# Spreading the position arithmetic of a deformable convolution between its taps

## The chip, the cores and the metric

The kernel runs on one core of one Trainium2 chip. Its engines are TensorE (PE in the profile; PEld is its weight load), VectorE (DVE), ScalarE (ACT), GpSimd (POOL) and SyncE (SP), which here only starts DMAs. The metric is the device time of one execution in microseconds, lower is better. Before the change it is 16,689.37 us, the median of three runs from 16,679.99 to 16,696.37.

## The reference

Four layers are applied one after the other to an array x of 8 images, 64 channels, 128 x 128 pixels, in float32, each as `x = x + layer(groupnorm(x))`. Layer 0 is a modulated deformable 3 x 3 convolution, layer 1 a plain 3 x 3 convolution, layer 2 a two-directional state-space scan, layer 3 a nearest-neighbour block. The change touches layer 0 alone:

```python
offset = conv2d(x, wh, bh, 0, p) + conv2d(x, wv, bv, p, 0)     # 1x15 and 15x1
mask = sigmoid(conv2d(x, wm, bm, 1, 1))                        # 3x3
y = deform_conv2d(x, offset, mask, wd, pad=1)
```

For each pixel and each of nine kernel points, `deform_conv2d` takes the pixel's position plus the offset, reads the four pixels around that place, weights them bilinearly (zero outside the image), multiplies by the mask, and sums over channels and kernel points with `wd`. A batch norm and a ReLU follow.

## The kernel before

Images are handled in pairs, two times 64 channels on 128 partitions, so there are four pairs `p`. Layer 0 first writes the normalized pair into a table in device memory (`fill`), in which one row holds a pixel and the one below it, so that one read of two neighbouring rows returns all four corners of a sampling place.

Then `deform` goes over 16 blocks `e` of eight image rows in each pair. A block is two calls of `sample` of four rows each, and a call is eight groups: four image rows (`m`) times two images (`i`). In one group a partition is a column of the row, and there are nine taps `k`, one for each kernel point. For each tap POOL issues one indirect DMA (L389), which gathers 128 pieces of 256 floats by the indices in `idx` into a `g` tile (four buffers); DVE multiplies them by the corner weights `wts` (L398) and sums the four corners (L399) into `sm`, which has two buffers. Five PE transposes (L403, L405) and two ACT copies (L406, L407) bring `sm` into channel order in `st`, and after eight groups ten PE products with `wd` (L412) give the four rows' result, which SP stores (L416). So a block has 16 groups and 144 gathers, and layer 0 has 64 blocks and 9,216 gathers.

Indices and weights of a block are made during the block before it. The generator `offsets` loads 22 image rows into `xe` (L311; two buffers), normalizes them on ACT (L312), and for each half of the block makes 33 shifted products on PE into `po` (L323), adds the bias on ACT (L333), transposes back (L336) and copies the result into `off` on DVE (L337). It gives way (`yield`) after every sixth product and after each copy. Then `positions` computes from `off`, with 17 DVE operations and one ACT sigmoid (L350 to L372), the clipped positions, their whole and fractional parts, the index `idx` (L364), and the four corner weights (L372). Before the change it is an ordinary function that issues all of these in one go.

What runs between the groups is set by `work`, which `sample` calls after each group. It takes one step of `near`, the `offsets` generator of the next block, and at each third call one step of `far`: the setup of later layers, and statistics and table of the next pair. What is left of `near` runs at the end of the block, what is left of `far` before the last block of a pair. This order of emission goes to a planner, which gives each engine an in-order queue; it keeps to the order of emission as far as operands and buffers are ready in its own estimate, and moves single instructions past each other where they aren't.

The layers after this one (`rest`) start when the last block is done and are not touched.

Of the kernel before, what the change touches and what calls it, by code (L numbers as in the profile page):

```python
# [41 lines left out]
class Net:  # L42
# [134 lines left out]
    def deform(self):  # L177
# [6 lines left out]
        with ExitStack() as ctx:  # L184
# [11 lines left out]
            with tc.tile_pool(name="a_setup", bufs=1) as sp:  # L196
                zeros = sp.tile([P, 2 * PW], F32, name="zeros")
                nc.gpsimd.memset(zeros, 0.0)
                for table in (t for pair in tables for t in pair):
                    flat = table.rearrange("a b q -> a (b q)")  # L200
                    n = LINE * PW // P
# [58 lines left out]
            ready = {}  # L260
# [44 lines left out]
            def offsets(p, e):  # L305

                r, nb = norms[p]
                lo, hi = max(0, 8 * e - 7), min(H, 8 * e + 15)
                xe = ep.tile([P, 22, H], F32, tag="xe", name=f"xe{p}_{e}")
                xf = xe.rearrange("p h w -> p (h w)")[:, 0 : (hi - lo) * H]  # L310
                nc.sync.dma_start(xf, self.x[p * P : (p + 1) * P, lo * H : hi * H])  # L311
                nc.scalar.activation(xf, xf, AF.Identity, bias=nb, scale=r)  # L312
                off = offp.tile([P, 3, 8, 18], F32, tag="off", name=f"off{p}_{e}")
                for g in (2 * e, 2 * e + 1):
                    po = ps_conv.tile([54, 4, H], F32, tag="po", name=f"po{p}_{g}")
                    used = []
                    for t, (dy, dx) in enumerate(taps):
                        r0, r1 = max(0, -dy - 4 * g), min(4, H - dy - 4 * g)
                        if r0 < r1:
                            used.append((t, dy, dx, r0, r1, max(0, -dx), min(H, H - dx)))  # L320
                    for n, (t, dy, dx, r0, r1, c0, c1) in enumerate(used):
                        row = 4 * g + dy - lo
                        nc.tensor.matmul(  # L323
                            po[:, r0:r1, c0:c1],
                            lhsT=wt[:, t, :],
                            rhs=xe[:, row + r0 : row + r1, c0 + dx : c1 + dx],
                            start=n == 0,
                            stop=n == len(used) - 1,
                        )
                        if n % 6 == 5:  # L330
                            yield
                    ob = op.tile([54, 4, H], F32, tag="ob", name=f"ob{p}_{g}")
                    nc.scalar.activation(ob, po, AF.Identity, bias=bias, scale=1.0)  # L333
                    tp = ps_t.tile([P, 4, 3, 18], F32, tag="tp", name=f"to{p}_{g}")
                    for m in range(4):
                        nc.tensor.transpose(tp[:, m].rearrange("p d n -> p (d n)"), ob[:, m, :], self.ident[0:54, 0:54])  # L336
                    nc.vector.tensor_copy(off[:, :, 4 * (g % 2) : 4 * (g % 2) + 4, :].rearrange("p d r n -> p r d n"), tp)  # L337
                    yield
                ready[p, e] = positions(p, e, off)
                yield  # L340

            def positions(p, e, off):

                n = 8 * 18
                h0 = 8 * e
                pos = op.tile([P, 2, n], F32, tag="pos", name=f"pos{p}_{e}")
                cell = op.tile([P, 2, n], F32, tag="cell", name=f"cell{p}_{e}")
                up = op.tile([P, 2, n], F32, tag="up", name=f"up{p}_{e}")
                o = off.rearrange("p d r n -> p d (r n)")
                nc.vector.scalar_tensor_tensor(pos[:, 0], base_y, float(h0), o[:, 0], ALU.add, ALU.add)  # L350
                nc.vector.tensor_add(pos[:, 1], base_x, o[:, 1])

                nc.vector.tensor_scalar(pos, pos, -2.0, float(H), ALU.max, ALU.min)  # L353
                whole = up.bitcast(I32)
                nc.vector.tensor_copy(whole, pos)
                nc.vector.tensor_copy(cell, whole)
                nc.vector.tensor_tensor(up, cell, pos, ALU.is_gt)
                nc.vector.tensor_sub(cell, cell, up)

                nc.vector.tensor_sub(pos, pos, cell)  # L360
                nc.vector.tensor_scalar(up, pos, -1.0, 1.0, ALU.mult, ALU.add)
                idx = wp.tile([P, n], I32, tag="idx", name=f"idx{p}_{e}")
                nc.vector.scalar_tensor_tensor(cell[:, 0], cell[:, 0], float(LINE), cell[:, 1], ALU.mult, ALU.add)
                nc.vector.tensor_scalar_add(idx, cell[:, 0], float(2 * LINE + 2))  # L364
                mask = o[:, 2]
                nc.scalar.activation(mask, mask, AF.Sigmoid)
                nc.vector.tensor_mul(pos[:, 0], pos[:, 0], mask)
                nc.vector.tensor_mul(up[:, 0], up[:, 0], mask)
                w = wtp.tile([P, n, 2, 2], F32, tag="wts", name=f"wts{p}_{e}")
                for b, wx in ((0, up), (1, pos)):  # L370
                    for a, wy in ((0, up), (1, pos)):
                        nc.vector.tensor_mul(w[:, :, b, a], wx[:, 1], wy[:, 0])  # L372
                w = w.rearrange("p n b a -> p n (b a)")
                wts = [w[:, 0 : n // 2], w[:, n // 2 :]]
                return idx, wts

            def sample(p, g, table, idx, wts, work):

                yp = ps_y.tile([P, CH], F32, tag="yp", name=f"yp{p}_{g}")
                flat = [table[i].rearrange("a b q -> (a b) q") for i in range(2)]  # L380
                st = [stp.tile([P, 5, CH], F32, tag="st", name=f"s{p}_{g}_{i}") for i in range(2)]
                for m in range(4):
                    for i in range(2):
                        n0 = m * 18 + 9 * i
                        t = gp.tile([P, 9, 4, C], F32, tag="g", name=f"g{p}_{g}_{i}_{m}")
                        tq = t.rearrange("p k q c -> p k (q c)")
                        for k in range(9):
                            at = (g % 2) * 72 + n0 + k
                            nc.gpsimd.indirect_dma_start(  # L389
                                out=tq[:, k, :],  # L390
                                out_offset=None,
                                in_=flat[i],
                                in_offset=bass.IndirectOffsetOnAxis(ap=idx[:, at : at + 1], axis=0),
                            )
                        sm = wp.tile([P, 9, C], F32, tag="sm", name=f"sm{p}_{g}_{i}_{m}")
                        for k in range(9):
                            w = wts[:, n0 + k, :].unsqueeze(2).to_broadcast([P, 4, C])
                            nc.vector.tensor_mul(t[:, k], t[:, k], w)  # L398
                            nc.vector.tensor_reduce(sm[:, k], t[:, k].rearrange("p q c -> p c q"), axis=mybir.AxisListType.X, op=ALU.add)  # L399
                        sm = sm.rearrange("p k c -> p (k c)")  # L400
                        sp = ps_s.tile([P, 4, P], F32, tag="sp", name=f"sp{p}_{g}_{i}_{m}")
                        for j in range(4):
                            nc.tensor.transpose(sp[:, j, :], sm[:, j * P : (j + 1) * P], self.ident)  # L403
                        s1 = ps_s1.tile([C, P], F32, tag="s1", name=f"s1{p}_{g}_{i}_{m}")
                        nc.tensor.transpose(s1, sm[:, 4 * P :], self.ident)  # L405
                        nc.scalar.copy(st[i][:, 0:4, m * P : (m + 1) * P], sp)  # L406
                        nc.scalar.copy(st[i][0:C, 4, m * P : (m + 1) * P], s1)  # L407
                        work()
                for j in range(5):
                    rows = P if j < 4 else C  # L410
                    for i in range(2):
                        nc.tensor.matmul(yp[i * C : (i + 1) * C, :], lhsT=wd[0:rows, j, :], rhs=st[i][0:rows, j, :], start=j == 0, stop=j == 4)  # L412
                nc.vector.bn_stats(self.ystat[:, p * NCH + g, :], yp)
                ys = op.tile([P, CH], F32, tag="ys", name=f"ys{p}_{g}")
                nc.scalar.copy(ys, yp)
                nc.sync.dma_start(self.y[p][:, g * CH : (g + 1) * CH], ys)  # L416
# [10 lines left out]
            for p in range(self.npair):  # L427
# [4 lines left out]
                for e in range(NCH // 2):  # L432
# [4 lines left out]
                    count = [0]  # L437

                    def work(near=near, far=far, count=count):
                        count[0] += 1  # L440
                        next(near, None)
                        if count[0] % 3 == 0:
                            next(far, None)

                    idx, wts = ready.pop((p, e))
# [933 lines left out]
```

## Time and profile before

| What | Value |
|---|---|
| median of three runs | 16,689.37 us |
| the profiled execution's own time | 16,687.07 us |
| its span | 16,685.0 us |
| start to the first gather | 168 us |
| first gather to last gather (layer 0) | 11,716 us: POOL busy 8,910, DVE 8,600, PE 7,144, ACT 1,240 |
| after the last gather | 4,801 us |
| gathers (L389) | 9,216, median 946 ns, mean 967 ns, data landing 2.7 us after the issue |
| granted TensorE clock | 0.79 of full speed in layer 0, 0.91 after it |

The span is the time from the first to the last instruction of one profiled execution. An engine's busy time is the sum of its instructions' records, and issuing of ordinary DMAs isn't counted in it; the gathers on POOL are. Busy times of different engines overlap and can't be added. In a group's row, the idle time is what its engine spent without work just before these instructions, with the cause that ended most of it; "issue" is a pause that nothing in the profile explains as a wait.

### The profile page before, as it was taken

The page shows a single profiled execution, that of the slowest core. Times are in us where ns is not written, and L with a number is a line of the kernel's source. Part 1 is how long each engine was busy: PE and PEld are TensorE (multiplying, and loading weights), DVE is VectorE, ACT ScalarE, POOL GpSimd, SP SyncE. Part 2 cuts the span into 40 slices and gives each one's busy share as a digit, 9 for nine tenths or more (in the row PEclk, how much of TensorE's full clock was granted, in tenths as well). Part 3 has the DMA queues.
Part 4 walks back from the last instruction along what each step waited for, and adds up shares of the span by engine and source line. Part 5 has one row for each costly group of instructions (what it writes and reads, how often), then busy time and mean ns, then how long its engine had stood idle before and what let it go on. Part 6 is the DMA issues. An engine that isn't in the chain of part 4 may idle for free. (4 is left out here: it accounts for less than half of the span.)

```text
span 16685.0 us, 119663 instructions
## 1 busy us (share of the span) xinstructions
PE 11226.6 (67%) x31864; PEld 4101.4 (25%) x31864; DVE 11600.4 (70%) x27208; ACT 2990.4 (18%) x5596; POOL 10394.8 (62%) x10484
## 2 busy tenths in 40 slices
PE   6766565756576655667566566663489888988896
PEld 1211111111111111111111111111144344444443
DVE  6777777777777777777777777777557557566566
ACT  1101111111110011111000110100144243243342
POOL 4777777777777777777777777777434134043142
PEclk9987787878787787878778788776689899999897
DMA  5334444444433344443333333333322433424223
GB/s 172 120 115 128 133 130 135 136 131 134 137 120 112 114 129 130 135 131 120 112 114 113 118 115 114 118 110 108 118 67 68 148 77 104 112 78 133 85 67 103
DMA packets 900631, 1937.61 MB, mean 116 GB/s; under 512 B 199916, under 2 KB 435828, under 8 KB 876404
## 3 DMA queue, kind: packets, MB, share of 16 engines
q0 software_dynamic: 442368, 1208.55, 24.4%
q1 hardware_dynamic: 383204, 684.00, 13.4%
q10 hardware_dynamic: 74384, 37.40, 1.1%
q8 instruction: 260, 4.26, 0.1%
q14 instruction: 415, 3.40, 0.1%
HBM read 1544.92 MB, written 208.10 MB: 105 GB/s over the span
## 5 line engine op out<-in xcount | busy, mean ns | idle before, releaser
L389 POOL DMA_INDIRECT g<-table,idx x9216 | 8908.4, 967 | 2809.5 <-issue 2613.6
L398 DVE TENSOR_TENSOR g<-g,wts 128x256 f32<-128x256 f32 x9216 | 3818.1, 420 | 3101.9 <-DMA g<-table,idx 3084.0
L399 DVE TENSOR_REDUCE sm<-g 128x64 f32<-128x256 f32 x9216 | 4988.3, 580 | 0.8 <-DVE pos L353 0.2
L323 PE MATMUL po<-xe,wt 128*54 128x512 f32 (+3 forms) x8384 | 4734.9, 676 | 44.4 <-ACT ob L333 42.5
L403 PE MATMUL sp<-ident,sm 128*128 128x128 f32 x4096 | 1525.1, 377 | 4117.6 <-DVE sm L399 4100.3
L403 PEld LDWEIGHTS sp<-ident,sm 128*128 128x128 f32 x4096 | 626.2, 155 | 6897.7 <-DVE sm L399 4964.4
L406 ACT COPY s<-sp 128x512 f32<-128x512 f32 x1024 | 600.0, 586 | 8514.1 <-PE sp L403 8514.1
L323 PEld LDWEIGHTS po<-xe,wt 128*54 128x54 f32 x8384 | 929.9, 140 | 1417.2 <-issue 1069.3
L840 POOL COPY l_yb<-ln_y 128x512 f32<-128x512 f32 x128 | 79.1, 659 | 1303.9 <-PE l1v L834 1161.4
L412 PE MATMUL yp<-s,wd 128*64 128x512 f32 (+1 forms) x2560 | 808.1, 652 | 12.6 <-ACT s L406 12.6
L1206 POOL TENSOR_TENSOR u<-u,v 128x512 f32<-128x512 f32 x256 | 330.7, 1292 | 697.4 <-DVE v L1205 519.7
L563 PE MATMUL c<-room,l_w 128*64 128x508 f32 (+1 forms) x3072 | 741.3, 597 | 21.1 <-DMA room<-nx 14.9
L1298 POOL TENSOR_TENSOR ms<-ms,ln_y 128x512 f32<-128x512 f32 x256 | 278.4, 1107 | 738.8 <-DVE ln_y L119 706.7
L1188 ACT ACTIVATE fx<-room,ln_b,ln_g 128x512 f32<-128x512 f32 x512 | 639.2, 1293 | 116.2 <-DMA in<-fx 97.9
L405 PE MATMUL s<-ident,sm 128*64 128x128 f32 x1024 | 345.9, 338 | 363.1 <-DVE sm L399 336.1
L1221 DVE TENSOR_TENSOR_SCAN z<-tabs,z,u 128x256 f32<-128x256 f32 x512 | 444.9, 902 | 208.3 <-POOL u L1206 192.9
L1199 PE MATMUL pv<-in,tabs 128*128 128x512 f32 x1024 | 537.2, 649 | 46.2 <-DVE u L1205 46.2
L1268 PE MATMUL py<-x,outs 128*128 128x512 f32 x1024 | 506.0, 599 | 4.6 <-POOL x L1253 4.2
L1268 PE MATMUL py<-in,outs 128*128 128x512 f32 x1024 | 505.7, 606 | 1.6 <-ACT h L1270 1.2
L1285 PE MATMUL pc<-outs,h 128*128 128x256 f32 x2048 | 498.9, 394 | 9.9 <-DVE h L1271 8.8
L1253 POOL TENSOR_TENSOR x<-x,xt 128x512 f32<-128x512 f32 x256 | 350.6, 1370 | 126.3 <-DVE xt L1252 126.0
L1285 PEld LDWEIGHTS pc<-outs,h 128*128 128x128 f32 x2048 | 382.5, 195 | 168.7 <-issue 65.4
(406 smaller groups left out, 10008.7 us busy)
## 6 DMA issues: line engine op xcount, KB each, us to landing
g<-table,idx POOLq DMA_INDIRECT x9216, 2.7
in<-fx SPq DMA_DIRECT2D x1024, 128.0 KB
xe<-in_x_dram SPq DMA_DIRECT2D x56, 1408.0 KB
table<-q SPq DMA_DIRECT2D x256, 256.0 KB
xs<-in_x_dram SPq DMA_DIRECT2D x32, 1024.0 KB
xt<-in_x_dram SPq DMA_DIRECT2D x32, 1024.0 KB
y<-ys SPq DMA_DIRECT2D x128, 256.0 KB
room<-in_x_dram SPq DMA_DIRECT2D x64, 512.0 KB
```

The costliest lines, as they stand in the source:

```text
L323: nc.tensor.matmul(po[:, r0:r1, c0:c1], lhsT=wt[:, t, :], rhs=xe[:, row + r0 : row + r1, c0 + dx : c1 + dx], start=n == 0, stop=n == len(u ...
L389: nc.gpsimd.indirect_dma_start(out=tq[:, k, :], out_offset=None, in_=flat[i], in_offset=bass.IndirectOffsetOnAxis(ap=idx[:, at : at + 1], ...
L398: nc.vector.tensor_mul(t[:, k], t[:, k], w)
L399: nc.vector.tensor_reduce(sm[:, k], t[:, k].rearrange("p q c -> p c q"), axis=mybir.AxisListType.X, op=ALU.add)
L403: nc.tensor.transpose(sp[:, j, :], sm[:, j * P : (j + 1) * P], self.ident)
L406: nc.scalar.copy(st[i][:, 0:4, m * P : (m + 1) * P], sp)
L412: nc.tensor.matmul(yp[i * C : (i + 1) * C, :], lhsT=wd[0:rows, j, :], rhs=st[i][0:rows, j, :], start=j == 0, stop=j == 4)
L563: nc.tensor.matmul(o, lhsT=lt, rhs=mv, start=k < 2, stop=k >= len(calls) - 2)
L1188: nc.scalar.activation(fx[:, e].rearrange("p h (o m) -> p h o m", m=self.INNER), src[:, e::2], AF.Identity, bias=w["ln1_b"], scale=w["ln1_g"])
L1199: nc.tensor.matmul(pv, lhsT=tabs[:, at : at + P], rhs=fx[:, :, h, :], start=h == 0, stop=h == 1)
L1268: nc.tensor.matmul(py, lhsT=lt, rhs=mv, start=n == 0, stop=n == len(calls) - 1)
L1285: nc.tensor.matmul(pc[:, i], lhsT=hs[:, h, i, m * P : (m + 1) * P], rhs=self.outs[:, CEN : MIX + P], start=True, stop=True)
```

## The change

`positions` becomes a generator that gives way after each of its DVE operations, 17 times in all, and `offsets` runs it with `yield from`. `offsets` itself gives way after every third product, no longer every sixth. `sample` no longer calls `work` after each group but after taps 2, 5 and 8 of each group, inside the loop over taps: 48 calls in a block where there were 16. `far` takes a step at each ninth call in place of each third. No operation is added, removed or altered.

```diff
-                        if n % 6 == 5:
+                        if n % 3 == 2:
                             yield
...
-                ready[p, e] = positions(p, e, off)
+                ready[p, e] = yield from positions(p, e, off)
                 yield
...
                 nc.vector.scalar_tensor_tensor(pos[:, 0], base_y, float(h0), o[:, 0], ALU.add, ALU.add)
+                yield
                 nc.vector.tensor_add(pos[:, 1], base_x, o[:, 1])
+                yield
...
                 for b, wx in ((0, up), (1, pos)):
                     for a, wy in ((0, up), (1, pos)):
                         nc.vector.tensor_mul(w[:, :, b, a], wx[:, 1], wy[:, 0])
+                        yield
...
                             nc.vector.tensor_mul(t[:, k], t[:, k], w)
                             nc.vector.tensor_reduce(sm[:, k], t[:, k].rearrange("p q c -> p c q"), axis=mybir.AxisListType.X, op=ALU.add)
+                            if k % 3 == 2:
+                                work()
...
                         nc.scalar.copy(st[i][0:C, 4, m * P : (m + 1) * P], s1)
-                        work()
...
-                        if count[0] % 3 == 0:
+                        if count[0] % 9 == 0:
                             next(far, None)
```

More of the change, by code (lines that the diff above doesn't have):

```diff
@@ L350, in positions @@
                 nc.vector.scalar_tensor_tensor(pos[:, 0], base_y, float(h0), o[:, 0], ALU.add, ALU.add)
+                yield
                 nc.vector.tensor_add(pos[:, 1], base_x, o[:, 1])
+                yield
                 nc.vector.tensor_scalar(pos, pos, -2.0, float(H), ALU.max, ALU.min)
+                yield
                 whole = up.bitcast(I32)
                 nc.vector.tensor_copy(whole, pos)
+                yield
                 nc.vector.tensor_copy(cell, whole)
+                yield
                 nc.vector.tensor_tensor(up, cell, pos, ALU.is_gt)
+                yield
                 nc.vector.tensor_sub(cell, cell, up)
+                yield
                 nc.vector.tensor_sub(pos, pos, cell)
+                yield
                 nc.vector.tensor_scalar(up, pos, -1.0, 1.0, ALU.mult, ALU.add)
+                yield
                 idx = wp.tile([P, n], I32, tag="idx", name=f"idx{p}_{e}")
                 nc.vector.scalar_tensor_tensor(cell[:, 0], cell[:, 0], float(LINE), cell[:, 1], ALU.mult, ALU.add)
+                yield
                 nc.vector.tensor_scalar_add(idx, cell[:, 0], float(2 * LINE + 2))
+                yield
                 mask = o[:, 2]
@@ L367, in positions @@
                 nc.vector.tensor_mul(pos[:, 0], pos[:, 0], mask)
+                yield
                 nc.vector.tensor_mul(up[:, 0], up[:, 0], mask)
+                yield
                 w = wtp.tile([P, n, 2, 2], F32, tag="wts", name=f"wts{p}_{e}")
@@ L372, in positions @@
                         nc.vector.tensor_mul(w[:, :, b, a], wx[:, 1], wy[:, 0])
+                        yield
                 w = w.rearrange("p n b a -> p n (b a)")
```

## The prediction

> **What bounds the kernel now.** The chip's granted clock and the slices of the page come first: gathers run from the start to slice 29 of 40, and in all of these slices both POOL and DVE show 7 tenths. The question is which of the two waits for the other. The costliest groups of the page (line, engine, operation, out<-in, count, busy us and mean ns, idle before and who ended it):
>
> ```profile
> L389 POOL DMA_INDIRECT g<-table,idx x9216 | 8908.4, 967 | 2809.5 <-issue 2613.6
> L398 DVE TENSOR_TENSOR g<-g,wts 128x256 f32<-128x256 f32 x9216 | 3818.1, 420 | 3101.9 <-DMA g<-table,idx 3084.0
> L399 DVE TENSOR_REDUCE sm<-g 128x64 f32<-128x256 f32 x9216 | 4988.3, 580 | 0.8 <-DVE pos L353 0.2
> ```
>
> DVE waits 3,084 us for gathered data; POOL waits for nearly nothing but its own issue. 8908.4 + 2809.5 = 11,718 us is the stage: the source view of L389 starts the first gather at 167.9 and the last at 11,883.7. That view's waits, by cause:
>
> ```profile
>   issue: 2613.6, 8581
>   DVE sm L399: 142.7, 470
>   DVE g L398: 31.5, 104
> ```
>
> 8,581 of the waits are plain issue of 0.3 us, and the same 0.3 us stands before gathers put down to DVE, so no gather waits for a buffer. POOL is the bound, end to end, and only a shorter gather can shorten the stage. The median gather is 0.946 us, the mean 0.967. I took all 9,215 distances between gather starts from POOL's timeline: the common one is 1.25 us, 9,215 x 1.25 = 11,519, the stage is 197 us longer. So 197 us, 1.2%, is all that can be won here. Where it lies: one block is 144 gathers (16 groups of 9). Groups 14 and 15 of all 64 blocks together carry 114.3 us of it, each other group on average 0.0925 us per block. POOL's timeline in one block at these groups (start, us, idle before):
>
> ```profile
> 6006.01 0.95 POOL L389 DMA_INDIRECT g<-table,idx  x1 [0.30 <-issue]
> 6007.26 0.98 POOL L389 DMA_INDIRECT g<-table,idx  x1 [0.30 <-issue]
> 6008.55 1.33 POOL L389 DMA_INDIRECT g<-table,idx  x1 [0.30 <-issue]
> 6010.18 1.00 POOL L389 DMA_INDIRECT g<-table,idx  x1 [0.30 <-issue]
> 6011.48 1.15 POOL L389 DMA_INDIRECT g<-table,idx  x1 [0.30 <-issue]
> 6012.94 1.37 POOL L389 DMA_INDIRECT g<-table,idx  x1 [0.30 <-DVE sm L399]
> ```
>
> and DVE's at the same time:
>
> ```profile
> 6008.21 0.42 DVE L398 TENSOR_TENSOR g<-g,wts 128x256 f32<-128x256 f32 x1
> 6008.54 0.30 DVE L361 TENSOR_SCALAR up<-pos 128x288 f32<-128x288 f32 x1
> 6008.76 0.30 DVE L363 SCALAR_TENSOR_TENSOR cell<-cell 128x144 f32<-128x144 f32 x1
> ...
> 6010.58 0.57 DVE L399 TENSOR_REDUCE sm<-g 128x64 f32<-128x256 f32 x1
> 6011.07 0.75 DVE L398 TENSOR_TENSOR g<-g,wts 128x256 f32<-128x256 f32 x2
> 6011.74 1.08 DVE L399 TENSOR_REDUCE sm<-g 128x64 f32<-128x256 f32 x2
> 6012.74 0.75 DVE L398 TENSOR_TENSOR g<-g,wts 128x256 f32<-128x256 f32 x2
> ```
>
> The reader is to see two things. While nine position operations run in a row (6008.54 to 6010.58), a gather takes 1.33 us; in other blocks one takes 2.36 to 2.88. Then DVE is behind and runs taps without a pause, two multiplies and two reduces in 1.66 us, and gathers lengthen to DVE's rhythm. In quiet stretches DVE pauses some 0.7 us before every second multiply, and gathers stay at 0.95.
>
> **What the Trainium skill says.** "SBUF — State Buffer", section "Who interferes with whom": a VectorE instruction with two SBUF inputs, or one in a two-port mode (casts and tensor_scalar can be), shares a port pair with GpSimd under an exclusive lock, and a tensor_reduce doesn't. The trace agrees: of 8,359 gathers with a distance under 1.27 us, 5% start while such a DVE operation runs; of 550 with 1.35 to 1.8 us, all do. From phase 0.25 to 0.75 us of a gather they do no harm: there the multiplies lie in most ordinary gathers. "Perfetto Trace Analysis", section "DMA Instruction — SWDGE (GPSIMD)", says a gather's record ends when its descriptors are written, not when data lands; here data land 2.7 us (median) after the issue, so POOL's record is the right measure of its pace. No page prices the order of DVE instructions.
>
> **The change, part by part.**
>
> (a) Positions, 17 DVE operations per block (L350 to L372), are neither added nor removed. By the source views of their lines, medians: 301+298+312+296+300+446+450+446+301+298+226+299+300+412+424+426+424 = 5.96 us per block; start to start in the block above they took 7.64 us less four taps' 3.3, so 4.3 us, 0.25 each. DVE's timeline now has the first eight alternating with taps and the last nine in one run, all within 7.6 us, in which POOL makes six gathers. So DVE falls 4.3 / 1.25, over three gathers, behind; each gather of the catch-up is 0.41 us long in excess (1.66 - 1.25), and the run itself costs up to 1.4 us. Price now: 114.3 - 2 x 64 x 0.0925 = 102.5 us, 1.6 per block. After: one operation per three taps. Three gathers are 3.75 us; three taps cost DVE 3 x 0.83 = 2.5, and one operation 0.25, so DVE still pauses 1.0 us in each three and never falls behind. By phase: multiply at 0.25 to 0.67, two reduces, multiply at 0.35 to 0.75 of the next gather, the operation behind it ends by about 1.1, short of the next start at 1.25. Hence no delay. I take 0.01 us for each of 17 x 64 operations, as gathers over lone operations of L355 to L357 show (0.001 to 0.006): 11 us. The bounds: zero, and 0.15 (gathers over L358 with L360, at the end of a run), 163 us.
>
> (b) The conv of the next block (L323) yields after 3 products rather than 6, in calls three times as frequent: its result is copied (L337) at calls 12 and 24 of 48, the ends of groups 4 and 8, where it was groups 6 and 12. Nothing added. L323's 4,734.9 us over 4,192 products (two records each) are 1.13 us, so 33 take 37 us; four groups are 45 us and hold besides 20 transposes of 0.35 and, at a call's end, the ten products of L412 (5 us): 49 us. PE would run 4 us late between groups 4 and 8 and catch up after 12; the trace has such a conv in 44 us already (6188 to 6233). The lag is covered: two sm buffers give one group, 11.25 us, before DVE waits, and four g buffers about three more before POOL does. L399 waited 0.8 us in the whole run. Zero; if the cover were gone, each us per block would cost 64.
>
> (c) The sigmoid on ACT (L366) depends on L337 alone, which lies at call 24; its user L367 is 12 calls later. idx is written at about call 35, group 12, where it was written after group 13; POOL needs it for group 17 and can't pass group 16 without it. Weights come at call 42, group 14, needed by DVE at 17. Nothing is late. All 42 steps fit in 48 calls.
>
> (d) Far work keeps its places (every ninth of 48 calls for every third of 16), moved from behind a group's transposes to before them. Its DMAs (L267, L287, L301 on SP) keep their count. The xe load (L311, 1,408 KB, SP) goes when the conv has read an older xe, so some three groups earlier, around group 13. It is behind late gathers such as a 4.72 us pause of DVE at 6050; the catch-up that follows would now meet some four position operations: 4 x 0.25 / 0.83 taps, each 0.41 us, 0.5 us per block in the worst case, 32 us; I take 5, as most such loads cause far less. SP's queue is empty most of the time.
>
> Sum: -102.5 + 11 + 5 = -86.5, so 16,687 (the profiled execution; span 16,685) gives 16,600. The median shown, 16,689, is 2 us off; 0.2%, 33 us, is about what a measurement of this kernel can tell from no change.
>
> **Rivals.**
>
> 1. The planner that orders each engine's queue packs the operations together again, and the change doesn't do what it says. For it: operations emitted in one go now alternate with taps, so emission doesn't decide alone. Against: L337 and L350 start at the group ends where they are emitted. Time 16,689, 16,660 to 16,715 if half is packed or one run grows.
> 2. Slower: operations in DVE's pauses land on gather starts. At 0.15 us for each, 163 - 102 = +61: 16,750. It decides from 102.5 / 1,088 = 0.094 us per operation; over 0.2% slower from 0.125. For it: multiplies are in step with gathers because data release them, position operations wait for no data. Against: the phases above.
> 3. PE becomes the bound between groups 4 and 12 and DVE waits for sm or sp. A lag of 45 us would be needed before POOL stops; at 50, 5 x 64 = 320, so about 16,900. Unlikely.
> 4. The other catch-ups go as well: up to 197 us, 16,490. Against: those 83 us follow late gathers, which the change leaves.
>
> **How the numbers follow.** Forecast 70% (16,565 to 16,650 on its own), rival 1 17%, rival 2 8%, rival 3 3%, rival 4 2%. Faster: forecast, rival 4 and a little of rival 1, 0.74; slower: rivals 2 and 3, and a little of 1, 0.12; same 0.14. The range, 16,560 to 16,700, leaves out rivals 2, 3 and 4, the end of rival 1 and a few in a hundred of the forecast.
>
> **What would show it.** Right: the L389 mean falls from 967 to about 958 ns at unchanged median, groups 14 and 15 are like the others, no gather takes over 2 us, the last gather starts near 11,797, and what follows it keeps 4,801 us. Wrong: operations of L361 to L372 in one run; gathers of 1.35 us at many places of groups 9 to 14; DVE waiting for PE at L399; POOL waiting for idx.

## The result, and the profile after

The changed kernel takes 16,598.36 us (median of five runs, 16,596.21 to 16,615.03) against 16,689.37 us (five runs, 16,673.80 to 16,696.37): a ratio of 0.995 with a 95% interval of 0.9939 to 0.996, 91 us less. The profiled execution has a span of 16,594.3 us, where it was 16,685.0.

The costliest groups of the page of the changed kernel; L389, L398 and L399 are now L405, L414 and L415:

```profile
L405 POOL DMA_INDIRECT g<-table,idx x9216 | 8834.7, 959 | 2809.4 <-issue 2635.5
L414 DVE TENSOR_TENSOR g<-g,wts 128x256 f32<-128x256 f32 x9216 | 3830.9, 420 | 3000.2 <-DMA g<-table,idx 2967.7
L415 DVE TENSOR_REDUCE sm<-g 128x64 f32<-128x256 f32 x9216 | 5014.0, 579 | 0.5
```

The mean gather fell from 967 to 959 ns, which is 74 us over 9,216 of them, and the pauses between gathers stayed at 2,809 us. The source view of L405 (minimum, median and longest gather, first and last start) and its causes of waiting:

```profile
L405 POOL DMA_INDIRECT g<-table,idx x9216: 942/946/1697, 167.2 to 11809.5; - x197
  issue: 2635.5, 8653
  DVE sm L415: 111.2, 366
```

The median is the same 946 ns; the longest gather fell from 2,878 to 1,697 ns. POOL is still the bound, and no new wait took the place of the time that went. POOL's timeline in one block (group 11), where the position operations now run:

```profile
5937.47 0.95 POOL L405 DMA_INDIRECT g<-table,idx  x1 [0.30 <-issue]
5938.72 0.94 POOL L405 DMA_INDIRECT g<-table,idx  x1 [0.30 <-issue]
5939.96 0.95 POOL L405 DMA_INDIRECT g<-table,idx  x1 [0.30 <-issue]
5941.21 0.95 POOL L405 DMA_INDIRECT g<-table,idx  x1 [0.30 <-issue]
```

and DVE's timeline at the same time:

```profile
5938.99 0.42 DVE L414 TENSOR_TENSOR g<-g,wts 128x256 f32<-128x256 f32 x1
5939.32 0.45 DVE L369 TENSOR_TENSOR pos<-pos,cell 128x288 f32<-128x288 f32 x1
5939.69 0.59 DVE L415 TENSOR_REDUCE sm<-g 128x64 f32<-128x256 f32 x1
5940.19 0.42 DVE L414 TENSOR_TENSOR g<-g,wts 128x256 f32<-128x256 f32 x1
5941.53 0.42 DVE L414 TENSOR_TENSOR g<-g,wts 128x256 f32<-128x256 f32 x1 [0.92 <-DMA g<-table,idx]
5941.88 1.08 DVE L415 TENSOR_REDUCE sm<-g 128x64 f32<-128x256 f32 x2
5942.87 0.42 DVE L414 TENSOR_TENSOR g<-g,wts 128x256 f32<-128x256 f32 x1
5943.20 0.34 DVE L371 TENSOR_SCALAR up<-pos 128x288 f32<-128x288 f32 x1
```

One operation sits behind a multiply in each three taps, DVE still pauses (0.92 us here), and the gathers keep their 0.95 us. This holds for the whole trace: of the spans from one gather's start to the next, 1,066 hold the start of one position operation and only 3 that of more than one.

Where the 91 us went, by stage of the two profiled executions:

| Stage | before | after | difference |
|---|---|---|---|
| start to the first gather | 167.9 | 167.2 | -0.7 |
| first to last gather | 11,715.9 | 11,642.2 | -73.7 |
| after the last gather | 4,801.2 | 4,784.8 | -16.4 |

The last row holds no instruction that the change touches. 11 us of it lie at one place, the norm ahead of the first scan layer (`first_norm`). From its first product (L870 before) to the first use of its result (L862) the kernel before took 26.9 us (12,135.5 to 12,162.4), the changed one 15.6. One pair of products in PE's timeline before:

```profile
12144.13 2.05 PE L870 MATMUL pc<-room,center_r 128*128 128x512 f32 x2
```

and after, the same pair of products:

```profile
12066.97 1.10 PE L887 MATMUL pc<-room,center_r 128*128 128x512 f32 x2
```

The granted clock in these stretches was 0.50 before (12,140 to 12,145) and 1.00 after (12,065 to 12,070), and two further executions below took 15.6 and 15.5 us here. They have 4,787.5 and 4,794.6 us in the whole stage, and ten on other chips, of kernels with the same layers in it, 4,782 to 4,826. So executions differ here by more than the 16 us from chip to chip and kernel to kernel, and nothing shows that these 16 are an effect of the change. The gathers' 73.7 us come back in the control below (77.8).

### The profile page after: what moved, and what is told of

Same layout as the page of the kernel before. It is cut to its first block, busy times and chain, and to the rows that moved or that the text cites. A ratio compares the mean times of both kernels' runs of the same rounds, so it can differ in the third digit from the quotient of the medians.

```text
span 16594.3 us, 119574 instructions
## 1 busy us (share of the span) xinstructions
PE 11150.0 (67%) x31864; PEld 4099.0 (25%) x31864; DVE 11621.1 (70%) x27208; ACT 3000.5 (18%) x5596; POOL 10321.0 (62%) x10484
## 5 line engine op out<-in xcount | busy, mean ns | idle before, releaser
L405 POOL DMA_INDIRECT g<-table,idx x9216 | 8834.7, 959 | 2809.4 <-issue 2635.5
L414 DVE TENSOR_TENSOR g<-g,wts 128x256 f32<-128x256 f32 x9216 | 3830.9, 420 | 3000.2 <-DMA g<-table,idx 2967.7
L415 DVE TENSOR_REDUCE sm<-g 128x64 f32<-128x256 f32 x9216 | 5014.0, 579 | 0.5
L323 PE MATMUL po<-xe,wt 128*54 128x512 f32 (+3 forms) x8384 | 4576.1, 656 | 34.3 <-ACT ob L333 32.2
L429 PE MATMUL yp<-s,wd 128*64 128x512 f32 (+1 forms) x2560 | 906.6, 718 | 30.0 <-ACT s L424 29.8
L580 PE MATMUL c<-room,l_w 128*64 128x508 f32 (+1 forms) x3072 | 742.1, 597 | 21.6 <-DMA room<-nx 15.5
```

The costliest lines, as they stand in the source:

```text
L323: nc.tensor.matmul(po[:, r0:r1, c0:c1], lhsT=wt[:, t, :], rhs=xe[:, row + r0 : row + r1, c0 + dx : c1 + dx], start=n == 0, stop=n == len(u ...
L405: nc.gpsimd.indirect_dma_start(out=tq[:, k, :], out_offset=None, in_=flat[i], in_offset=bass.IndirectOffsetOnAxis(ap=idx[:, at : at + 1], ...
L580: nc.tensor.matmul(o, lhsT=lt, rhs=mv, start=k < 2, stop=k >= len(calls) - 2)
```

## The experiments

The measure used below is the excess of the gathers: the sum of all 9,215 distances from one gather's start to the next, less 1.25 us for each. It is 197.0 us in the kernel before and 123.5 in the changed kernel.

The traces show at which gathers it lies. Of the kernel before, 3,738 gathers start while DVE is idle and 4,069 while only a reduce runs: together they carry 1 us of excess. The 1,108 that start while a multiply of the taps runs carry 185 us, and the 300 at other DVE operations 11. In the changed kernel the multiplies have 985 starts and 117 us, the other operations 253 and 5. So the long gathers are, with few exceptions, ones that start during a multiply. If late or crowded transfers alone made gathers long, those that start during reduces should be long too.

### The changed kernel and the bunched positions, side by side

First the changed kernel once more, as a control.

> The changed kernel itself beside the kernel before, because the six runs so far met a chip on which the kernel before takes some 18,750 us and DVE, PE and ACT stand still for tens of microseconds at a time. If this chip is like the first: 16,590 to 16,615 against 16,675 to 16,700, excess of the gathers 110 to 135 us. If it is like the two others: the standstills decide, and the change is lost in them, ratio 0.99 to 1.01.

Measured: 16,600.06 us against 16,688.68, ratio 0.9953 (0.9936 to 0.9969), excess 119.4 us. It repeats.

Then, on the same chip, the position operations put together again, while the 48 calls and the finer conv stay:

```diff
-                ready[p, e] = yield from positions(p, e, off)
+                ready[p, e] = positions(p, e, off)
...
                 nc.vector.tensor_add(pos[:, 1], base_x, o[:, 1])
-                yield
```

(and so for all 17).

> The changed kernel with the 17 position operations in one go again, as in the first experiment. Like the first chip: theory, excess back to about 200 us with some 100 us of it at groups 9 and 10, time 16,675 to 16,695; rival (finer conv made the gain), 16,595 to 16,615. Like the two others: within 1% of the kernel before, and slower than the changed kernel by 50 to 100 us.

Measured: 16,665.25 us against 16,688.68 for the kernel before, ratio 0.9988 (0.9981 to 0.9995); 65 us slower than the changed kernel. DVE's timeline of this kernel has the old run again (six operations left out at the dots):

```profile
5941.77 0.33 DVE L363 TENSOR_SCALAR up<-pos 128x288 f32<-128x288 f32 x1
5942.02 0.29 DVE L365 SCALAR_TENSOR_TENSOR cell<-cell 128x144 f32<-128x144 f32 x1
5942.23 0.29 DVE L369 TENSOR_TENSOR pos<-pos,off 128x144 f32<-128x144 f32 x1
...
5943.86 0.57 DVE L401 TENSOR_REDUCE sm<-g 128x64 f32<-128x256 f32 x1
5944.36 0.75 DVE L400 TENSOR_TENSOR g<-g,wts 128x256 f32<-128x256 f32 x2
```

and POOL's gathers at the same time are longer than 0.95 us again, if less than in the block that the prediction showed:

```profile
5942.27 1.07 POOL L391 DMA_INDIRECT g<-table,idx  x1 [0.30 <-issue]
5943.65 1.07 POOL L391 DMA_INDIRECT g<-table,idx  x1 [0.30 <-issue]
5945.02 0.94 POOL L391 DMA_INDIRECT g<-table,idx  x1 [0.30 <-issue]
```

The excess by place in the block (us over all 64 blocks, from the four POOL timelines):

| Groups of the block | before | changed | changed, control | bunched again |
|---|---|---|---|---|
| 1 to 8 | 50.2 | 42.5 | 46.5 | 38.6 |
| 9 and 10 | 7.8 | 18.0 | 16.3 | 88.5 |
| 11 to 13 | 19.5 | 37.8 | 33.8 | 33.9 |
| 14 and 15 | 114.3 | 10.1 | 8.8 | 8.8 |
| 16 | 5.2 | 15.2 | 13.8 | 12.5 |
| sum | 197.0 | 123.6 | 119.2 | 182.3 |

The bunch moved from groups 14 and 15 to 9 and 10, behind the place where the finer conv now ends, and a price moved with it: 88.5 against 16.3 us, 72 us. This settles the main cause: spacing the same 17 operations is worth 63 us of excess and 65 us of time here. It also splits off the rest: the 48 calls and the finer conv alone give 0.12%, 23 us by the medians, 15 of them in the gathers. The theory had given them nothing; its 16,675 to 16,695 was missed by 10 us at its lower end.

At its old place the bunch had cost more: groups 14 and 15 had 114.3 us where the control has 8.8, 105 us against the 72 at the new place. The traces name a candidate for the difference. In the kernel before, 26 of DVE's pauses of over 1.5 us that follow an `xe` load lie at groups 13 and 14, just ahead of the bunch; in the bunched kernel 2 lie at groups 9 and 10. That late data ahead of the bunch make it dearer is not shown by a run of its own.

The table answers one more question. In groups 11 to 16, in which about twelve of a block's 17 spaced operations start, the spaced and the bunched kernel have the same excess (56.4 and 55.2). Outside groups 14 and 15, these groups had 24.7 us before and have 47.6 in the control and 46.4 in the bunched kernel. So the growth is not that of the spaced operations; it came with the finer conv or with what that moves. A count by single gathers gives the operations a small price of their own: in groups 9 to 16 of the changed kernel, gathers that a position operation touches (it runs at their start, or starts before the next one) have 0.028 us of excess on average, the others 0.014. If all of that difference is theirs, it is 17 us over the whole kernel, 16 in the control, or 0.016 us for each operation.

### Ten kernels on chips with standstills

The ten other runs met chips on which the kernel before itself takes 18,743 to 18,818 us. There it is not the gathers alone that set the time. The timeline of one of them (the kernel before with additional reduces, in the middle of a block) shows why. The bracket holds the idle time before the instruction, and the dots stand for rows left out:

```profile
2565.52 1.08 DVE L402 TENSOR_REDUCE sm<-g 128x64 f32<-128x256 f32 x2
...
2602.45 0.95 POOL L392 DMA_INDIRECT g<-table,idx  x1 [0.30 <-issue]
2603.70 0.94 POOL L392 DMA_INDIRECT g<-table,idx  x1 [0.30 <-issue]
2603.86 0.58 ACT L409 COPY s<-sp 128x512 f32<-128x512 f32 x1 [43.83 <-issue]
2604.95 0.94 POOL L392 DMA_INDIRECT g<-table,idx  x1 [0.30 <-issue]
...
2607.32 0.29 DVE L295 COPY q<-tp 128x128 f32<-128x128 f32 x1 [40.72 <-issue]
2607.67 1.11 PE L291 MATMUL tp<-ident,xt 128*128 128x128 f32 x4 [40.62 <-issue]
```

DVE, PE and ACT stand still together, here for some 40 us, with no wait that the profile explains. POOL goes on until its four buffers are full, and then DVE works off a backlog without a pause, which is the very state that lengthens gathers. Pauses of DVE of over 20 us number 44 to 89 in the stage of gathers of these runs, with medians of 27 to 32 us. The durations of the gathers alone are then about 760 to 1,030 us over the median in sum, and POOL's idle time beyond the usual pauses another 1,160 to 1,950; a difference of 60 to 100 us can't be found in that. These runs are told for what they still show.

The first, the bunched kernel again:

> The changed kernel, with the 17 position operations issued in one go again; the 48 calls and the finer conv stay. Theory (DVE falls behind at the bunch): the excess of the gathers over 1.25 us returns to about 200 us, now at groups 9 and 10, stage 11,715 us, time 16,675 to 16,695. Rival (the finer conv, the earlier xe loads or the 48 calls made the gain): time stays at 16,595 to 16,615.

Measured: 18,953 us against 18,778, ratio 1.0096 (1.0065 to 1.0126).

The split without the finer conv: the conv takes a step at each third call, and positions give way after each second operation.

```diff
-                        if n % 3 == 2:
+                        if n % 6 == 5:
                             yield
+                            yield
+                            yield
```

(Not shown: two more `yield`s at the start of `offsets` and two after its first copy, and the `yield`s of `positions` that are left out.)

> 48 calls, but the conv takes a step at every third call only, so it keeps its old places at group ends up to group 12; the position operations go two to a call from group 13 on. Theory: two operations are 0.5 us in 3.75 us, below DVE's pause of 1.25 us, so the excess is 95 to 125 us and the time 16,585 to 16,620. Rival (the finer conv made the gain): 16,670 to 16,700.

Measured: 18,850 us against the same 18,778, ratio 1.0035 (1.0014 to 1.0057). The spaced version is 103 us below the bunched one on the same chip, as the theory would have it, but both are above the kernel before, as it would not. It can't be counted as a confirmation. The bunched kernel is 0.12% faster than the kernel before on the one kind of chip and 1% slower on the other.

Four operations to a call (the `yield` after all but the 4th, 8th and 12th operation removed):

> The changed kernel with four position operations to a call (4, 4, 4 and 5). Theory: 1.0 us of DVE in 3.75 us is still below the pause of 1.25 us, but each run of four can meet a gather's start: excess 125 to 165 us, where the changed kernel has 123 and the kernel before 197. If only the number of operations in a row counted, groups 9 and 10 would hold half of the old 104 us.

Measured: one run of 18,873 us against 18,778. Inconclusive.

The positions begun 13 calls later:

```diff
+LATE = 13
...
+                for _ in range(LATE):
+                    yield
                 ready[p, e] = yield from positions(p, e, off)
```

> The changed kernel with the positions begun 13 calls later, so that idx is written by the 48th call, after group 16, and the weights at the block's end. Theory: the first gather of a block now waits for idx; the last gather's data land 2.7 us after its issue, then two taps and the operation follow, about 4.0 us after its start where the next gather would start at 1.25: 2.8 us per block, 175 to 220 us in all, time 16,770 to 16,830, with POOL waiting for idx. If the lead of POOL over DVE hid it: 16,600.

Measured: one run of 19,215 us against 18,778, 437 us more, and here the cause stands out of the disturbance. The source view of the gathers of this kernel, its causes of waiting:

```profile
  issue: 2648.8, 8690
  DVE idx L379: 990.6, 59
  DVE sm L418: 971.5, 258
```

POOL waits for idx in 59 blocks, 991 us in all; the median pause in front of a block's first gather is 15.9 us (2.2 to 34.3), where 2.8 had been expected. The estimate assumed that DVE follows each gather at once. Here DVE is behind by 12 gathers in the median and by 25 at most when a block's last gather ends, and what is written last in a block comes as late as DVE is. That an index written at the block's end is exposed is shown; its price on an undisturbed chip is not.

One more multiply of two tensors behind each position operation, measured on two chips (one of the 17 places is shown; the added result isn't used):

```diff
                 nc.vector.tensor_add(pos[:, 1], base_x, o[:, 1])
+                nc.vector.tensor_mul(spare, base_y, base_x)
                 yield
```

> The changed kernel with one multiply of two SBUF tensors (128x144, result not used) behind each of the 17 position operations. Theory: 17 operations of 0.22 us fit into DVE's pauses; 0.01 to 0.03 us each over 1,088, so the excess rises from 123 to 135 to 155 us. Rival (each operation in a pause lands on a gather's start, 0.1 to 0.15 us): 230 to 290 us.

> The changed kernel with one multiply of two SBUF tensors (128x144, result not used) behind each of the 17 position operations. Theory: 17 operations of 0.22 us more per block fit into DVE's pauses, 0.01 to 0.03 us each over 1,088: excess from 120 to 130 to 155 us, time 16,605 to 16,640. Rival (each operation in a pause lands on a gather's start, 0.1 to 0.15 us): excess 230 to 290 us, time 16,705 to 16,770.

Measured: 18,753 us against 18,743 on one chip and 18,842 against 18,818 on another. 1,088 additional operations cost 10 and 24 us by single runs, which is within what these chips scatter. It fits the small price found above and proves nothing alone.

Nine reduces, and in another kernel nine multiplies, behind the bunch of the kernel before:

```diff
                         nc.vector.tensor_mul(w[:, :, b, a], wx[:, 1], wy[:, 0])
+                spare = op.tile([P, n], F32, tag="spare", name=f"spare{p}_{e}")
+                for _ in range(9):
+                    nc.vector.tensor_reduce(spare, pos.rearrange("p d n -> p (d n)").rearrange("p (a b) -> p a b", b=2), axis=mybir.AxisListType.X, op=ALU.add)
```

(in the other kernel `nc.vector.tensor_mul(spare, pos, up)` in place of the reduce, with `spare` twice as wide).

> The kernel before with nine reduces of one SBUF tensor (288 elements, result not used) behind the positions, some 3.3 us more of DVE in the bunch. Theory: DVE falls another 2.7 taps behind, each 0.41 us of excess, 1.1 us per block: the excess rises from 197 to about 250 to 280 us. If only operations that share the port with POOL count: it stays at 197 to 210.

> The kernel before with nine multiplies of two SBUF tensors (288 elements, result not used) behind the positions, the same 3.3 us of DVE. Theory: the backlog of the reduces plus a gather held through the run: 1 to 2.5 us per block more than with the reduces, excess 310 to 440 us. If only the backlog counts: the same as with the reduces.

Measured: one run each, 18,671 and 18,695 us, against 18,743. Both are below the kernel that does less, so nothing can be read from them. How much of the bunch's price is the run of operations itself and how much is the catch-up behind it can be told by place alone, from the traces above. In the kernel before, the 414 gathers between the first and the last position operation of their blocks carry 60 us of excess, and the 20 gathers behind these in each block 65; in the bunched kernel of the section above it is 44 and 60. So the two are of like size. How much the second would be without the first was not measured.

Smaller loads, to shorten what is left of the excess. First `xe` with 14 of its 22 rows copied on ACT from the block before; then also the rows for the table in pieces of four, which is not shown:

```diff
-                nc.sync.dma_start(xf, self.x[p * P : (p + 1) * P, lo * H : hi * H])
...
+                    nc.scalar.copy(xe[:, 0:kept, :], old[:, at0 : at0 + kept, :])
...
+                nc.sync.dma_start(xf, self.x[p * P : (p + 1) * P, (lo + kept) * H : hi * H])
```

> The changed kernel, with 14 of the 22 rows of xe copied on ACT from the block before, so that the load is 8 rows (512 KB) where it was 22 (1,408 KB). Theory (what is left of the excess are catch-ups after gathers that landed late beside a large load): DVE's pauses after xe loads, 215 us in 60, fall to some 80 us, the excess from 123 to about 85 to 95 us, time 16,560 to 16,575. Rival (pauses come from other transfers): 16,590 to 16,605.

> The changed kernel with 14 of the 22 rows of xe copied on ACT from the block before (load of 512 KB where it was 1,408), and the rows for the table loaded four at a time (256 KB) where it was sixteen. Theory (what is left of the excess are catch-ups after gathers that land late beside large loads): DVE's pauses over 1.5 us, 445 us in 166 in the changed kernel, fall below 250 us, the excess from 120 to about 60 to 85 us, time 16,535 to 16,570. Rival (the position operations in the pauses make the surplus of groups 9 to 16): excess 100 to 120 us, time 16,585 to 16,605. A chip with the standstills tells neither.

Measured: 18,766 us against 18,743, ratio 1.0011 (1.0000 to 1.0022), and 18,949 against 18,818, ratio 1.007 (1.0046 to 1.0094). On these chips smaller loads win nothing. Whether they would where gathers set the time is not known. The reason to try them still stands in the trace of the changed kernel: of its 166 pauses of DVE over 1.5 us before a gather's data, 63 begin within 10 us of an xe load's issue, 224 of 445 us, and the twelve gathers from such a pause on carry 47 us of the excess. Outside groups 14 and 15 these gathers have 43 us, 43 in the control and 37 in the bunched kernel, where the kernel before has 22.

## Why the prediction was right

The forecast was 16,600 us and the median is 16,598. That they agree to 2 us is luck; step by step the prediction was less exact than that.

- **The bound.** Right. POOL's gathers run end to end in both kernels, only their length changed, and the stage shrank by the excess that went, 73.7 us.
- **Part (a), the bunch.** Right in mechanism and in the sum at its place: groups 14 and 15 went from 114.3 to 10.1 us, against an expected 102.5 taken off. But not all of the 102.5 is the price of the bunch as such. At groups 9 and 10 the same bunch costs 72 us; the rest goes already when the finer conv moves it, which was part (b). The explanation by phases fits: nearly all excess lies at gathers that start during a multiply, and there are 123 fewer of these after the change. The working asked for up to 1.4 us in the run and 1.4 in the catch-up of each block; by place it is about 0.9 and 1.0, ordinary excess included. The block shown is an unusual one: its run starts in group 13, as in 6 of the 64, and at 122 to 127 of a block's gathers (group 14, the start of 15) in most.
- **The lone operations and the moved loads.** Mis-sized as a sum: 11 and 5 us were taken, and the groups other than 14 and 15 grew from 82.7 to 113.4 us, 31 more. The lone operations have 17 of these by the count of gathers and none by the table; the 11 lie between. The moved loads are where it was too small: the load goes some three groups earlier, as forecast, and the excess behind it, outside groups 14 and 15, grew by 22 us, within the bound of 32 that was given. It grew by 16 in the bunched kernel too, so most of it comes without position operations in the catch-up, which the working had made the reason. That the load is the cause is not shown, since the runs meant to test it said nothing.
- **Part (b), the finer conv.** Hidden on PE, as argued: L415 waits 0.5 us in the whole run, and PE makes nobody late. But "zero" was not exact: with the bunch left in, this part is worth 23 us by the medians, 15 of them in the gathers, because the bunch costs less at groups 9 and 10.
- **Part (c).** Right where it was used: no gather waits for idx. The late version shows, on a chip with standstills, that POOL does wait when idx is written last.
- **The stage after the last gather.** Forecast at 4,801 us, measured 4,784.8. This -16.4 us was not foreseen, and it makes up for the 13 us that the gathers fell short (73.7 against 86.5). 11 us of it are a stretch of lower granted clock in the profile of before. This is where the luck lies.
- **The rivals.** The first fell: one operation stands at every third tap, as emitted. The second needed over 0.094 us for each operation, and the count of gathers gives them 0.016. The third fell with L415's 0.5 us. The fourth fell: 123.5 us of excess are still there.

## What to carry to other kernels

Where GpSimd's gathers run end to end, look at the sum of what they exceed their median by, and at where in the loop it lies: here it was 1.2% of the kernel, and more than half of it in two of sixteen groups. An engine with a quarter of its time free can still cost the engine that sets the pace, when its side work comes in one piece and takes it out of step; the same work spread one operation to a pause was nearly free. Ask also during which of the other engine's operations the long ones start: here it was the multiplies, and hardly ever the reduces. Spread the work early enough that what the pacing engine needs next isn't the last thing written.

## What the runs showed of the hardware

That gathers care so little for DVE's reduces and so much for its multiplies stands in the counts above: 4,069 starts during reduces cost 1 us, 1,108 during multiplies 185. They are counts of what goes together. No run on a chip without standstills swaps the one operation for the other.

That PE, ACT and DVE stand still together for tens of microseconds, on some chips and not on others, was not expected. DVE's waits for which the profile names no instruction are under 1 us in the stage of gathers of the kernel before and of the changed kernel on the first chip, and 3,020 to 4,420 us in the ten runs above. The kernel before takes 12 to 13% longer there. The added time lies in the stage of the gathers: what follows the last gather takes 4,782 to 4,826 us in these ten runs, and 4,785 to 4,801 on the chips without standstills. POOL and the data transfers in flight go on meanwhile (107 GB/s from 2,579 to 2,590 us in the case shown, with PE, DVE and ACT at nothing). The mean granted clock is lower in these runs, 0.76 where it was 0.82 to 0.83; whether that is a cause or an effect is not shown, and no other cause was found.

The changed kernel itself was not run on such a chip. Seven of the eight versions with 48 calls in a block were measured 10 to 175 us slower there than the kernel before, the eighth (the late one) 437, four of the eight by single runs. So the 0.5% of this change is shown for chips without standstills alone.
